# A four-layer graph network on one core: other lengths, due times and look-ahead in the plan that orders its instructions

## The chip, the cores and the metric

The kernel runs on one core of a Trainium2 chip. The metric is the device time of one execution in microseconds (us). A core has five engines that run side by side: PE multiplies matrices (and transposes by multiplying with the identity), DVE and ACT work elementwise, POOL (GpSimd) too, more slowly, and SP only issues transfers (DMAs). Each engine takes its instructions strictly in the order in which the program puts them, and waits on semaphores for the others.

## The reference, cut to what matters

x holds 32 graphs of 512 nodes with 128 features. Four layers follow one another, each of this form:

```python
h = jnp.maximum(_layernorm(x, axis=-1), 0.0)
x = x + _L0_gnn_ref(h, adj, ...)      # then L1, L2, L3 in the same way
```

Layer 0 is an attention whose scores come from pairs of nodes (node 2m and 2m+1 give the score of entry m), so small columns of h must be moved between partitions. Layers 1 and 2 are attentions with a row score plus a column score, a leaky slope, a softmax and a product with h; layer 1 adds a product with the adjacency matrix, two norms and two dense products. Layer 3 multiplies by an attention matrix that depends only on adj and on one vector of weights: it is the same for all graphs and is computed once. The graphs are independent of each other; within a graph the four layers are a chain.

## The kernel before, in words

**Tiling.** A graph is held as 128 partitions by 4 chunks by 128 features. All 32 graphs stay in `xs` on the chip. Everything that depends on adj or on weights alone is made once: the opening block (adjacency transposed and turned into masks; lines 440 to 497), `prepare()` (layers 1 and 2: folded weights, centred rows, the adjacency with its diagonal) and `prepare_last()` (layer 3's matrix, `offT` and `adiag`, lines 1072 and on: masks at L1108, counts at L1126, membership `in_row` at L1185, products at L1212, L1225 and L1259, the diagonal at L1297).

**The plan.** The order of the instructions is not that of the code. Each step is handed to `op(engine, length, emit, reads, writes, ...)` with a length in microseconds that the author measured or guessed, and `Plan.run()` plays the whole kernel through as a list schedule: it keeps a clock for each engine, takes the operation that can begin first (within `SLACK`, the one with the earliest turn), emits it, and moves on. The emitted order is then fixed by dependencies. The plan's lengths are never seen by the chip; they only decide the order on each engine. Where they are wrong, an engine is made to wait at an instruction whose input is late, and everything behind it on that engine waits too.

**What the plan reckons.** An operation ends at its length, and its reader may begin `DELAY` later. A load of data holds a modelled bus for `load` microseconds; transfers take up some of eight lanes. When the plan sees PE idle for more than `PAUSE` it puts in filler transposes (`idle_products`, L334) that keep PE busy and compute nothing.

**Turns.** Each layer of each graph is a chain with a begin time: layer 0 of graph n, layer 1 of graph n-6, layer 2 of graph n-12 and layer 3 of graph n-16 take turns, `GAPS` apart; the first `AHEAD` chains are `RAMP` times further apart. `PREPARED` and `FILLED` give the two preparation blocks their begin and the step by which each operation's turn rises. `AHEAD` is also how many graphs' x are loaded before the first is worked on.

**Layer 0** (from line 690). `preln` takes statistics on DVE (L511, L513), the inverse deviation on POOL (L523, L525) and then normalizes either on ACT (L541 on DVE and L545 on ACT) for the first `EARLY` graphs, or on POOL (L556 on ACT and L560 on POOL) for the rest. PE transposes and projects (L595), ACT copies `h` out (L412). Then comes the row of four small transfers, `emit_pair` (L699): SP moves two score columns of `h` to `u`, 0.5 KB each. DVE reads `u` first at L737. Exponentials follow on ACT (L777), two scalings on DVE (L805, L806), a split on ACT and POOL (L819, L820) and PE's products (L834 to L847); DVE and POOL add the result to `xs` (L853, L855, L857).

**Small values** (`small`, L308) come from one pool, `sm`, with eight buffers for each name. The plan doesn't know of that limit. Among them are the norms' `mv`, `shift` and `rstd`.

Of the kernel before, what the change touches and what calls it, by code (L numbers as in the profile page):

```python
# [28 lines left out]
F32 = mybir.dt.float32  # L29
# [8 lines left out]
P = 128  # L38
# [5 lines left out]

OLD, KEPT = 4, 1

AHEAD = 6


PE, DVE, ACT, POOL, SP = "PE", "DVE", "ACT", "POOL", "SP"  # L50

DELAY = {PE: 0.22, DVE: 0.15, ACT: 0.22, POOL: 0.13, SP: 2.2}

HOLD = 0.05

# [3 lines left out]

STRETCH = 3.7  # L60

PREPARED, FILLED = (35.0, 1.2), (109.0, 1.5)

RAMP = 4.1

PAUSE = 0.6

EARLY = 8

GAPS, LAGS = (5.3, 12.0, 6.7, 5.4), (0, 6, 12, 16)  # L70

# [40 lines left out]
class Plan:  # L112
# [17 lines left out]
    def op(self, engine, length, emit, reads=(), writes=(), load=0.0, transfers=0, port=0):  # L130
        slots = list(dict.fromkeys(v.slot for v in (*reads, *writes) if v.slot is not None))
        k = len(self.chains) - 1
        op = Operation(engine, length, emit, k, slots)
        op.load, op.transfers, op.port = load, transfers, port
        for s in slots:
            s.users += 1
        needs = {}
        for v in reads:
            needs.update(dict.fromkeys(v.writers))
        for v in writes:  # L140
            needs.update(dict.fromkeys(v.writers))
            needs.update(dict.fromkeys(v.readers))
        for v in reads:
            v.readers.append(op)
        for v in writes:
            v.writers.append(op)
        for n in needs:
            n.after.append(op)
            if n.chain == k:
                op.way = max(op.way, n.way + n.length + DELAY[n.engine])  # L150
        count, beside, begin, _ = self.chains[k]
        turn = begin + STRETCH * op.way if beside is None else beside[0] + beside[1] * count
        op.turn = (turn, len(self.ops))
        op.missing = len(needs)
        self.chains[-1][0] += 1
        self.ops.append(op)

    def run(self):
        tc, nc = self.tc, self.tc.nc
        idle = dict.fromkeys(DELAY, 0.0)  # L160
        bus = 0.0
        lanes = [0.0] * LANES

        held = {DVE: [], POOL: []}
        ready = {e: [] for e in DELAY}
        for op in self.ops:
# [9 lines left out]
        for _ in range(len(self.ops)):  # L176
            while oldest < len(normal) and not left[normal[oldest]]:
                oldest += 1
            best = None
            for engine, ops in ready.items():  # L180
                could = []
                for op in ops:
                    k = op.chain
                    beside = self.chains[k][1] is not None
                    if not beside and order[k] >= oldest + WINDOW:
                        continue
                    begin = max(idle[engine], op.ready)
                    if op.transfers:
                        begin = max(begin, lanes[op.transfers - 1])
                    if op.port:  # L190
                        for a, b in held[POOL if engine is DVE else DVE]:
                            if a <= begin < b:
                                begin = b
                    new = [s for s in op.slots if s.tile is None]
                    rooms = {}
                    for s in new:
                        rooms[s.room] = rooms.get(s.room, 0) + 1
                    for room, n in rooms.items():
                        if len(room.free) < n + (room.reserve if beside else KEPT if order[k] >= oldest + OLD else 0):
                            begin = None  # L200
                            break
                        begin = max(begin, sorted(room.free)[n - 1])
                    if begin is not None:
                        could.append((begin, op.turn, op))
                if could:
                    first = min(c[0] for c in could)
                    c = min((c for c in could if c[0] <= first + SLACK), key=lambda c: c[1])
                    if best is None or c[0] < best[0]:
                        best = c
            assert best is not None, "no operation can begin"  # L210
            begin, _, op = best
            if op.engine is PE and idle[PE] and begin - idle[PE] > PAUSE:
                wanted = sum(s.tile is None and s.room is self.banks for s in op.slots)
                if sum(free <= idle[PE] for free in self.banks.free) > wanted:
                    self.idle_products(begin - idle[PE])
            ready[op.engine].remove(op)
            for s in op.slots:
                if s.tile is None:
                    s.room.free.remove(min(s.room.free))
                    s.tile = s.room.make(s.name)  # L220
            end = begin + op.length
            idle[op.engine] = end
            if op.port:
                piece = op.length / op.port
                held[op.engine] = [(begin + k * piece, begin + (k + 1) * piece - HOLD) for k in range(op.port)]
            done = end + DELAY[op.engine]
            if op.load:
                bus = max(done, bus) + op.load
                done = bus
            if op.transfers:  # L230
                lanes = lanes[op.transfers :] + [done] * op.transfers
            op.emit()
            traced = nc.cur_bb.bb.instructions
            while seen < len(traced):
                ins = traced[seen]
                seen += 1
                if ins.engine in last:
                    tc.add_manual_dep(
                        ins, last[ins.engine].name,
                        mybir.DependencyInfo(mybir.DependencyClass.NoSync, mybir.DependencyReason.DATA),  # L240
                        reason="the plan's order",
                    )
                last[ins.engine] = ins
            left[op.chain] -= 1
            for s in op.slots:
                s.users -= 1
                s.until = max(s.until, done)
                if not s.users:
                    s.room.free.append(s.until)
            for n in op.after:  # L250
                n.missing -= 1
                n.ready = max(n.ready, done)
                if not n.missing:
                    ready[n.engine].append(n)
# [3 lines left out]
def kernel(  # L258
# [35 lines left out]
    KE = NE // P  # L294
    assert F == P and C == 4 and NE % P == 0 and B >= AHEAD

    cp = ctx.enter_context(tc.tile_pool(name="const", bufs=1))
    ps = ctx.enter_context(tc.tile_pool(name="ps", bufs=8, space=bass.MemoryType.PSUM))
    sm = ctx.enter_context(tc.tile_pool(name="sm", bufs=8))

    def wide(t):

        return t.rearrange("p c f -> p (c f)")

    def blk(i):
        return bass.ts(i, P)

    def small(name, shape=(P, C)):  # L308
        return sm.tile(list(shape), F32, name=name, tag=name)

    def const(name, shape, dtype=F32):
        return cp.tile(list(shape), dtype, name=name)
# [16 lines left out]
    op = plan.op  # L329
# [30 lines left out]
    xs = const("xs", (P, B, C, P))  # L360
# [12 lines left out]
    bias = const("bias", (P, C, N))  # L373
# [23 lines left out]
    v_x = [Value() for _ in range(B)]  # L397
    v_adj = [Value() for _ in range(C)]
# [5 lines left out]
    def load(dst, src, writes, size=0.0):  # L404
        op(SP, 0.5, lambda: nc.sync.dma_start(dst(), src), writes=writes, load=size, transfers=1)

    def load_x(b):
        load(lambda: xs[:, b], x[b].rearrange("(c p) f -> p c f", p=P), [v_x[b]], 1.0)

    def copy_op(engine, length, dst, src, reads, writes):  # L410
        if engine is ACT:
# [28 lines left out]
    load(lambda: wt_o.t[:, 0, :], l0_wo, [wt_o], 0.25)  # L440
    load(lambda: att, l0_att.rearrange("(t p) o -> p (t o)", p=P), [v_att])
    for ib in range(C):
        load(lambda ib=ib: bias[:, ib, :], adj[blk(ib), :], [v_adj[ib]], 1.0)
    load(lambda: wts[:, W_S, :], l0_ws, [v_wts[W_S]], 0.25)
    for b in range(1, AHEAD):
        load_x(b)
# [240 lines left out]
    def layer0(b):  # L687
        hT, _ = preln(b, ACT if b < EARLY else POOL)
        if b + AHEAD < B:
            load_x(b + AHEAD)  # L690
        h = project_scored(hT, w0_ext, [v_w0, v_w0b])
        u = Value()
# [7 lines left out]
                        u.own[up * 64 : up * 64 + 64, :, k : k + 1], h[0].t[k:P:2, up:C:2, P + k : P + k + 1]  # L700
                    )

        op(SP, 1.8, emit_pair, h, [u], transfers=4)
        sc, ls = Value(), Value()

        def emit_sc():
# [618 lines left out]
    for n, (layer, gap, b) in enumerate(order):  # L1325
        plan.chain(gap * RAMP if n < AHEAD else gap, name=layer.__name__)
        layer(b)
# [34 lines left out]
```

## Time and profile before

| what | before |
|---|---|
| median of 3 runs | 1062.99 us (1062.88 to 1063.54) |
| profiled execution: its own time | 1063.87 us |
| profiled execution: span from first to last instruction | 1062.1 us |
| mean granted clock of PE | 0.996 |
| PE busy | 1041.7 us (98%) |
| DVE busy | 868.5 us (82%) |
| ACT, POOL busy | 780.5 us, 776.2 us |
| filler transposes | 150, 19.2 us of PE |
| chain that ended last | PE 88%, DVE 4%, POOL 3% |

A busy PE is not a PE at its peak: matmuls are pipelined, and their ends are modelled. So counts of matmuls in a stretch, and the gaps between their starts, say more than busy time. A group of instructions is named by line, engine, operation and tiles (out<-in); "idle before" says how long its engine had nothing to do just ahead of it, and whose event ended that. SPq is SP's queue; a transfer's line there is its issue, and the landing is a line of its own in the chain.

### The profile page before, as it was taken

How to read it: one execution, taken by the hardware profiler on the slowest of the kernel's cores; microseconds unless marked ns; L12 is line 12 of the kernel's file. 1: busy time of each engine (PE TensorE's matmuls, PEld its weight loads, DVE VectorE, ACT ScalarE, POOL GpSimd, SP SyncE). 2: the span in 40 equal slices, each digit the busy share in tenths (PEclk: the TensorE clock that was granted, in tenths of full speed). 3: DMA queues.
4: the chain of work that ended last, by engine and by line, in shares of the span. 5: the costliest groups of instructions: out<-in, count | busy, mean ns of one | idle time of the engine just before them, and what ended most of it. 6: DMA issues, size and time to landing. Idle time of an engine off the chain costs nothing.

```text
span 1062.1 us, 25166 instructions
## 1 busy us (share of the span) xinstructions
PE 1041.7 (98%) x8475; PEld 966.0 (91%) x8475; DVE 868.5 (82%) x3694; ACT 780.5 (73%) x2024; POOL 776.2 (73%) x1140
## 2 busy tenths in 40 slices
PE   7899999999999999999999999999999999999998
PEld 7789789989999999999999999999899999999997
DVE  7799999989988878888888888888888877766752
ACT  6768897789877777777877777787777777767751
POOL 4489577778787777787778778777877666576772
PEclk9899999999999999999999999999999999999999
DMA  6400000000010000000000000000000000000001
GB/s 181 96 12 2 1 2 21 2 12 11 2 31 2 21 21 21 22 21 12 2 12 11 12 12 12 11 2 11 12 11 11 11 11 11 11 22 11 22 24 37
DMA packets 56912, 20.49 MB, mean 19 GB/s; under 512 B 21584, under 2 KB 56272, under 8 KB 56784
## 3 DMA queue, kind: packets, MB, share of 16 engines
q1 hardware_dynamic: 56784, 18.90, 7.2%
q8 instruction: 67, 1.10, 0.5%
q14 instruction: 61, 0.50, 0.2%
HBM read 10.43 MB, written 8.39 MB: 18 GB/s over the span
## 4 chain that ended last, share of the span: by engine, by line
PE 88%; DVE 4%; POOL 3%; DMA 1%; SPq 1%; issue 1%; ACT 1%; POOLq 0%; DVEq 0%; ACTq 0%
PE po L675 20%; PE pt L421 16%; PE po L984 10%; PE pg L911 10%; PE proj L595 7%; PE po L837 5%; PE prow L421 3%; PE p L581 3%; PE pz L581 3%; PE px L581 3%; PE po L980 3%; PE po L842 2%; PE po L834 1%; PE po L847 1%; POOL xn L560 1%
## 5 line engine op out<-in xcount | busy, mean ns | idle before, releaser
L675 PE MATMUL po<-h,pT 128*128 128x128 f32 x2048 | 242.8, 275 | 0.8 <-DVE pT L664 0.8
L675 PEld LDWEIGHTS po<-h,pT 128*128 128x128 f32 x2048 | 236.4, 192 | 5.8 <-issue 4.1
L560 POOL TENSOR_SCALAR xn<-xs,shift,rstd 128x128 f32<-128x128 f32 x480 | 213.1, 459 | 2.8 <-DVE top L633 0.9
L655 ACT ACTIVATE y<-y,nmax 128x512 f32<-128x512 f32 x256 | 181.7, 714 | 5.3 <-DVE nmax L637 4.6
L525 POOL TENSOR_TENSOR rstd<-ve,mhalf 128x4 f32<-128x4 f32 x160 | 170.9, 1068 | 13.3
L622 DVE CUSTOM_DVE_ANT_0 y<-prow,bias 128x512 f32<-128x512 f32 x256 | 162.8, 683 | 1.6 <-PE prow L421 1.6
L984 PE MATMUL po<-h,offT 128*128 128x128 f32 x1024 | 135.4, 275 | 0.0
L911 PE MATMUL pg<-adjTe,hg 128*128 128x512 f32 x256 | 131.0, 593 | 0.0
L421 PE MATMUL pt<-ident,y 128*128 128x128 f32 x1024 | 130.2, 274 | 0.7 <-ACT hl L819 0.7
L421 PEld LDWEIGHTS pt<-ident,y 128*128 128x128 f32 x1024 | 115.1, 141 | 13.8 <-issue 8.5
L984 PEld LDWEIGHTS po<-h,offT 128*128 128x128 f32 x1024 | 124.6, 192 | 0.0
L511 DVE BATCH_NORM_STATS2 st<-xs 128x6 f32<-128x128 f32 x512 | 109.8, 277 | 7.2 <-POOL xs L962 4.5
L595 PEld LDWEIGHTS proj<-w_ext,hT 128*128 128x128 f32 x768 | 96.8, 192 | 19.0 <-issue 9.6
L595 PE MATMUL proj<-w_ext,hT 128*128 128x130 f32 x768 | 102.9, 277 | 1.4 <-ACT hT L570 1.3
L647 ACT ACTIVATE y<-y,src 128x512 f32<-128x512 f32 x128 | 84.6, 714 | 20.8 <-DVE rmax L622 19.6
L962 POOL TENSOR_TENSOR xs<-xs,em 128x512 f32<-128x512 f32 x32 | 42.0, 1312 | 76.8 <-DVE em L961 63.8
L956 POOL TENSOR_TENSOR v<-v,rows 128x512 f32<-128x512 f32 x32 | 40.9, 1279 | 72.4 <-DVE v L955 72.4
L570 ACT ACTIVATE hT<-pt 128x512 f32<-128x512 f32 x128 | 73.5, 589 | 25.3 <-PE pt L421 14.0
L647 ACT ACTIVATE y<-y,h 128x512 f32<-128x512 f32 x128 | 84.7, 714 | 7.9 <-DVE rmax L622 7.7
L664 DVE TENSOR_TENSOR pT<-pt,adjT 128x512 f32<-128x512 f32 x128 | 82.6, 681 | 5.7 <-PE pt L421 5.6
L421 PE MATMUL pt<-ident,xn 128*128 128x128 f32 x512 | 77.8, 274 | 1.5 <-POOL xn L560 1.3
L412 ACT COPY h<-proj 128x260 f32<-128x260 f32 x192 | 66.1, 371 | 13.4 <-PE proj L595 12.4
(204 smaller groups left out, 2302.3 us busy)
## 6 DMA issues: line engine op xcount, KB each, us to landing
xs<-in_x_dram SPq DMA_DIRECT2D x32, 256.0 KB, 4.0
out_dram<-yo SPq DMA_DIRECT2D x32, 256.0 KB, 2.3
u<-h SPq DMA_DIRECT2D x128, 0.5 KB, 1.8
bias<-in_adj_dram SPq DMA_DIRECT2D x4, 256.0 KB, 4.4
wts<-in_L_gnn_W_dram SPq DMA_DIRECT2D x3, 64.0 KB, 4.2
rows<-in_L_gnn_bias_dram SPq DMA_DIRECT2D x2, 64.0 KB, 3.7
wt_o<-L_gnn_others_weight_dram SPq DMA_DIRECT2D x1, 64.0 KB, 2.5
wts<-n_L_gnn_self_weight_dram SPq DMA_DIRECT2D x1, 64.0 KB, 4.5
```

Source lines behind the costliest of these rows:

```text
L421: nc.tensor.transpose(dst(k), src(k), ident)
L511: nc.vector.bn_stats(st[:, c, :], src(c))
L525: nc.gpsimd.tensor_tensor(rstd.own, ve, mhalf, ALU.pow)
L560: nc.gpsimd.tensor_scalar(xn.t[:, c, :], src[:, c, :], shift.own[:, c : c + 1], rstd.own[:, c : c + 1], ALU.add, ALU.mult,)
L581: nc.tensor.matmul(pt.t[:, c, :], lhsT=column(hT, c), rhs=w, start=True, stop=True)
L595: nc.tensor.matmul(p[:, c, :], lhsT=column(hT, 2 * k + c), rhs=w_ext, start=True, stop=True)
L622: nc.vector.tensor_tensor_reduce(wide(y[ib].t), wide(prow.t), bias[:, ib, :], 1.0, LOWEST, ALU.add, ALU.max, rmax.own[:, ib : ib + 1],)
L647: nc.scalar.activation(yw, yw, AF.Prelu, alpha=0.2, bias=src()[:, ib : ib + 1])
L655: nc.scalar.activation(yw, yw, AF.Exp, bias=nmax.own[:, ib : ib + 1], accum_out=ssum[0].own[:, ib : ib + 1])
L675: nc.tensor.matmul(po[ib].t[:, ib, :], lhsT=pT.t[:, jb, :], rhs=h[0].t[:, jb, 0:P], start=(jb == 0), stop=(jb == C - 1),)
L911: nc.tensor.matmul(wide(pg.t), lhsT=hg.t[:, nb, :], rhs=adjTe[:, nb, :], start=(nb == 0), stop=(nb == C - 1))
L984: nc.tensor.matmul(po[ib].t[:, ib, :], lhsT=offT[:, jb, blk(ib)], rhs=h1.t[:, jb, :], start=False, stop=(jb == C - 1),)
```

## The change

Nothing is computed differently. Seven numbers of the plan change, a delay of its own is given to rows of small transfers, and the norms' small values get a pool of their own:

```diff
-AHEAD = 6
+AHEAD = 5
+PAIRED = 1.4
-PREPARED, FILLED = (35.0, 1.2), (109.0, 1.5)
-
-RAMP = 4.1
+PREPARED, FILLED = (37.0, 1.3), (160.0, 1.3)
+
+RAMP = 4.7
-EARLY = 8
+EARLY = 12
...
-            done = end + DELAY[op.engine]
+            done = end + (PAIRED if op.transfers > 1 else DELAY[op.engine])
...
+    sm_norm = ctx.enter_context(tc.tile_pool(name="sm_norm", bufs=14))
...
-        return sm.tile(list(shape), F32, name=name, tag=name)
+        pool = sm_norm if name in ("shift", "mv", "rstd") else sm
+        return pool.tile(list(shape), F32, name=name, tag=name)
...
-        load(lambda: xs[:, b], x[b].rearrange("(c p) f -> p c f", p=P), [v_x[b]], 1.0)
+        load(lambda: xs[:, b], x[b].rearrange("(c p) f -> p c f", p=P), [v_x[b]], 1.35)
...
-        load(lambda ib=ib: bias[:, ib, :], adj[blk(ib), :], [v_adj[ib]], 1.0)
+        load(lambda ib=ib: bias[:, ib, :], adj[blk(ib), :], [v_adj[ib]], 1.35)
...
-        op(SP, 1.8, emit_pair, h, [u], transfers=4)
+        op(SP, 2.6, emit_pair, h, [u], transfers=4)
```

In the plan a row of four transfers holds SP for 2.6 us instead of 1.8, and its reader may begin 1.4 us after it instead of 2.2 (`DELAY[SP]`). A load of one graph's x, or of a quarter of the adjacency matrix, holds the modelled bus for 1.35 us instead of 1.0. Five graphs are loaded ahead instead of six. `EARLY` makes ACT normalize layer 0 for the first twelve graphs instead of eight. The two preparation blocks come due later. As the list schedule depends on all of these together, the order on every engine differs from early on; PE's last 312 rows of order (equal neighbours counted as one row) are the same in both programs.

## The prediction

> **What bounds the kernel now.** I read the busy shares first, then the windows of the span, then DVE's waits in the first 60 us, then the chain of waits there.
>
> ```profile
> span 1062.1 us, 25166 instructions
> PE 1041.7 (98%) x8475; PEld 966.0 (91%) x8475; DVE 868.5 (82%) x3694; ACT 780.5 (73%) x2024; POOL 776.2 (73%) x1140
> ```
>
> PE is busy for 98% of the span. The busy time includes 150 filler transposes (row L334: 19.2 us) and matmuls that are stretched, so the stretches matter more (columns: us, busy and count of PE, PEld, DVE, ACT, POOL; clock; DMA share; GB/s):
>
> ```profile
> 0.00:20.00 20.00, 14.64 (x114) 13.63 (x115) 13.84 (x88) 10.93 (x25) 9.47 (x22) 1.00 0.71 186
> 20.00:40.00 20.00, 17.75 (x151) 16.19 (x150) 16.82 (x107) 16.28 (x55) 8.64 (x13) 1.00 0.56 133
> 40.00:60.00 20.00, 16.78 (x111) 15.77 (x112) 15.01 (x91) 14.54 (x50) 10.95 (x18) 0.83 0.22 50
> 60.00:80.00 20.00, 18.73 (x153) 17.06 (x152) 18.10 (x84) 10.98 (x38) 19.32 (x31) 1.00 0.09 15
> 80.00:100.00 20.00, 20.00 (x178) 19.77 (x177) 19.56 (x93) 19.71 (x56) 19.49 (x33) 1.00 0.02 1
> 200.00:800.00 600.00, 599.98 (x4915) 556.74 (x4915) 511.42 (x2164) 456.91 (x1193) 465.28 (x681) 1.00 0.05 13
> ```
>
> From 200 to 800 us PE never rests and runs 8.2 matmuls a microsecond: nothing is to be had there. Before 80 us it runs 529 matmuls, 6.6 a microsecond, 131 of them fillers. The start is the only place with room, apart from the drain. Who is late there?
>
> ```profile
> DVE lt L737 <- DMA u<-h: 4.7, 3, 2.5
> DVE st L511 <- DMA xs<-in_x_dram: 2.6, 1, 2.6
> DVE edge L459 <- DMA bias<-in_adj_dram: 1.3, 1, 1.3
> ```
>
> ```profile
> 27.39 3.02 SPq L699 DMA_DIRECT2D u<-h  x4
> 33.99 2.55 SPq L699 DMA_DIRECT2D u<-h  x4
> 38.85 2.74 SPq L699 DMA_DIRECT2D u<-h  x4
> ```
>
> ```profile
> 40.98 3.28 DMA u<-h
> 44.38 0.16 DVE lt L737
> ```
>
> DVE stands still three times (0.91, 1.27, 2.55 us by its timeline) because the row of four small transfers of layer 0 (L699) lands later than the plan thought. SP needs 2.6 to 3.0 us to issue a row; the plan reckons 1.8.
>
> [...] 0.6 us of SP for each L699 transfer, then a median of 1.8 us to landing. [...] behind the wait of 2.55 us at 41.8 us DVE ran nothing. [...] The trace shows clock 0.83 in 40 to 60 us, after thin PE work. [...] here the start is DVE's and the rest PE's.
>
> **The yardstick.** I add up the queues in the order in which each built program puts them, every instruction at the mean of its row in this trace (PE at its cadence in a full stretch: 0.109 us a transpose pass, 0.223 for a two-pass 128-column matmul, 0.86 for a 512-column one of L911). Where PE waits for DVE's n-th instruction, DVE's sum up to n less PE's sum so far is DVE's lead; the largest lead plus DVE's own idle time is what PE loses. Before: PE's sum 1024.3 us; largest lead 11.4 us (120 us into PE's work, at about 145 us); DVE's idle by then 14.6 us. 1024.3 + 11.4 + 14.6 = 1050.3; the other 11.8 us to the span of 1062.1 are 4.4 us after the last matmul and small stalls that I carry over unchanged. The profiled execution took 1063.87 us (1.8 more than its span); the median is 1062.99, 0.9 above the span. I convert by adding 0.9.
>
> **The change, part by part.**
>
> *PAIRED 1.4, row of four 2.6 instead of 1.8; x and adjacency loads 1.35 instead of 1.0.* No instruction is added; the order changes. The plan's old sum for a row was 1.8 + 2.2 = 4.0 us and the new one 2.6 + 1.4 = 4.0, but SP is now held for 2.6, as measured. In SP's order there stood 18, 4 and 4 loads between the first rows; now 20, 3 and 3 (layer 3's own four loads stay among the first of these, so their rows wait behind them as before). At the measured 0.59 us a load (10.6 us for 18) the second row starts about 1.1 us later, near 28, and lands near 33. DVE's first reader of rows 2 to 6 now stands behind 29.7, 34.8, 38.9, 44.5 and 48.1 us of DVE work (before 25.2, 30.6, 35.0, 44.0, 62.3). With the unavoidable 5.6 us of idle at the start DVE gets there at 35, 40, 44.5, 50 and 54 us. By the same working the rows land at 33, 37, 41.5, 46.5 and 54: of 4.7 us of waiting about 0.3 is left. Gain 4.4 us. Bounds: nothing (a row whose h is late, as then DVE waits all the same) and 4.7. What is late next is PE's or ACT's hand-over around 80 us.
>
> *Fillers.* They follow from the plan: 131 in the start become 100 (19 in the drain stay). 31 x 0.109 = 3.4 us less in PE's queue: PE's sum is 1020.9. This is a gain only if nothing real waits there instead.
>
> *PREPARED, FILLED, RAMP, AHEAD.* They move layer 3's preparation back: in DVE's order the first in_row (L1185) stands behind 83.6 us of work, before 49.3; the last diagonal (L1297) behind 154.8, before 122.5. Graph work moves ahead of it. The same DVE work is merely spread, but DVE stays ahead of PE's needs for longer: the largest lead grows from 11.4 to 13.8 us and lies at 152 us of PE work instead of 120. Cost 2.4 us; and DVE's idle, which grew by 1.4 us between 145 and 178 us, counts up to the later point: cost 1.4 us. AHEAD 5 issues each x load one graph later; layer 0's first wait for x was only the first load (2.6 us), so zero. Cover: x(1) to x(4) are issued before 8 us, long before use. Without cover a load shows 4.0 us.
>
> *EARLY 12.* Four more norms of layer 0 go from POOL to ACT: POOL loses 16 x 0.444 = 7.1 us, ACT gains 16 x 0.409 less 4 x 0.205 = 5.7 us, DVE gets four shifts at 0.08 = 0.3 us (in PE's lead above). POOL was full from 60 to 100 us, ACT only in 80 to 100. DVE idled 2.9 us between 60 and 80, when POOL led the chain. I take no gain; bounds are 2.9 us gained and the loss in the rival below.
>
> *Own room of 14.* Before, ACT's shift waited 9.6 us for POOL's xn, three times, all beyond 200 us, where ACT has slack. So zero before; it keeps norms begun earlier from waiting for eight-deep room. Cover: PE's full queue. Bounds zero to 1 us gained in the start.
>
> *Drain.* PE's last 312 rows of order, from 791.5 us on, are the same in both. Zero.
>
> **Sum.** 1020.9 + 13.8 + (14.6 - 4.4 + 1.4) + 11.8 = 1058.1 us of span, 4.0 under 1062.1. With 0.9: **1059.0 us**. Low end of this case: POOL's 2.9 us also go, 1056; high end: half of the row waits stay, 1061.
>
> **Rivals.** A, larger gain (0.14): the row waits, POOL's 2.9 us and half of the 6.8 us of half-rate clock (at most 3.4 us) go together; 1059.0 - 2.9 - 2.5 = 1053.5. For it: POOL led the chain from 57 to 74 us; against it: DVE's larger lead hides PE's clock. B, nothing moves (0.22): the rows wait for h rather than for SP, and DVE idles 14.6 + 1.4 as before: 1059.0 + 4.4 = 1063.4. For it: the fourth reader's h depends on ACT's queue of exponentials; the orders name the same handovers. C, ACT becomes the bound (0.15, slower): four more norms of 1.6 us stand in ACT's queue before the products at 60.8 us of PE work, and ACT's sum there is 1.3 us above PE's. Before, ACT had idled 28.2 us by 80 us, since it waits for others. To keep my forecast it may idle 24. Each further microsecond is one of PE; from about 30 the kernel is slower. With 33: 60.8 + 1.3 + 33 puts PE at 95 us there, 34.3 us lost, and DVE's lead grows by another 0.5: 1020.9 + 34.8 + 11.8 = 1067.5, and 1068.4 with 0.9. Against it: ACT's idle came mostly from DVE's waits, which shrink.
>
> **Numbers.** Forecast 0.49, A 0.14, B 0.22, C 0.15. About 0.2% (2.1 us) is what a measurement of this kernel can tell from no change. Faster is under 1060.9: most of the forecast (0.46) and A, with a little of B (0.02): 0.62. Within 0.2%: B 0.17, forecast 0.03, C 0.02: 0.22. Slower: C 0.13 and B's upper part 0.03: 0.16. The range leaves out one in ten at each end: half of A below, most of C above: 1053 to 1066.
>
> **What would show it.** Right: DVE's waits for u under 1 us in the first 60; fewer than 110 fillers in the start; POOL under 18 of 20 us busy in 60 to 80; from about 90 us PE full. DVE at 98% up to about 180 us. Wrong: waits for u of 4 us or more, ACT waiting long for DVE's nmax or PE's proj in 40 to 80, or PE idle after 100 us.

## The result, and the profile after

| | before | after |
|---|---|---|
| median of 20 runs each | 1063.09 us (1061.44 to 1064.45) | 1065.45 us (1064.33 to 1066.53) |
| profiled execution: own time, span | 1063.87, 1062.1 us | 1065.6, 1063.9 us |
| filler transposes | 150 | 119 |
| one round of four layers, between 375 and 750 us | 31.15 us | 31.55 us |

The changed kernel takes 1.0022 times as long (95% interval 1.0016 to 1.0029): 0.22% slower. The interval lies above 1, and the difference is about the 0.2% that the prediction took as the least that can be told from no change. The forecast was 1059.0 us, faster.

The busy shares of the changed kernel tell nothing of a loss:

```profile
span 1063.9 us, 25092 instructions
PE 1043.8 (98%) x8444; PEld 960.4 (90%) x8444; DVE 886.4 (83%) x3698; ACT 789.0 (74%) x2036; POOL 773.4 (73%) x1124
```

Its windows are the first thing that does (columns as in the prediction):

```profile
0.00:20.00 20.00, 14.79 (x119) 14.00 (x119) 12.69 (x75) 8.21 (x17) 7.29 (x20) 1.00 0.63 166
20.00:40.00 20.00, 18.32 (x147) 15.84 (x145) 19.69 (x129) 18.81 (x62) 12.88 (x20) 1.00 0.64 149
40.00:60.00 20.00, 18.46 (x152) 17.09 (x152) 18.67 (x120) 18.30 (x66) 15.36 (x26) 1.00 0.20 42
60.00:80.00 20.00, 16.48 (x127) 15.08 (x126) 18.64 (x89) 18.38 (x56) 19.18 (x31) 0.94 0.07 15
80.00:100.00 20.00, 20.00 (x164) 18.81 (x164) 16.32 (x75) 11.27 (x31) 16.52 (x26) 0.98 0.04 2
200.00:800.00 600.00, 599.63 (x4874) 551.40 (x4873) 528.17 (x2159) 457.44 (x1188) 469.31 (x681) 1.00 0.06 13
```

The first 60 us are fuller on DVE (51.1 us of 60, before 45.7) and ACT (45.3, before 41.8). But in the last line PE runs 4874 matmuls, where it ran 4915 before, in the stretch where the prediction had seen nothing to be had or lost. PE's busy time there fell by only 0.35 us. The weight loads' (PEld) fell by 5.3 us, from 556.74 to 551.40. The trace shows how a short wait hides in PE's busy time. The first of eight matmuls of `p` (L585, at 514.47 us, more of it below) starts 0.55 us after the matmul ahead of it, where 0.43 us is usual; the record of that one, 0.59 us long, covers the gap. The first matmul's own record is 0.38 us instead of 0.275; its weight load starts with it, where those of the other seven start 0.11 us ahead of theirs. So the mean of `p` between 400 and 750 us is 288 ns, where it was 275, and no idle time shows.

DVE's waits in the start went as forecast. Of those for transfers in the first 60 us, the ones for `u` (4.7 us before) are gone; only these two are left:

```profile
DVE st L515 <- DMA xs<-in_x_dram: 2.6, 1, 2.6
DVE edge L463 <- DMA bias<-in_adj_dram: 1.4, 1, 1.4
```

To see where time goes in a PE that is always busy I count its *work*: each matmul at the usual distance to the next one (the 20th percentile for its kind in that trace), fillers left out. What is left of a window is loss. (With kinds taken by line, tiles and shape, the levels move by up to 3 us; the loss between 400 and 800 us comes out the same within 0.1 us.)

| PE's work done by (us) | 100 | 200 | 300 | 400 | 500 | 600 | 700 | 800 |
|---|---|---|---|---|---|---|---|---|
| before | 62.9 | 156.7 | 254.7 | 352.9 | 451.5 | 550.0 | 648.6 | 747.3 |
| after | 65.4 | 158.9 | 257.3 | 355.6 | 453.0 | 550.5 | 647.7 | 745.1 |

The changed kernel is 2.6 us ahead at 300 us and 2.2 us behind at 800. It gives back about 4.9 us between 400 and 800, evenly, since from there on the plan's order repeats: one round of layers 0 to 3. In the timeline of PE the same product comes back after 31.55 us:

```profile
499.81 0.39 PE L838 MATMUL po<-wts,hT 128*128 128x128 f32 x2
...
531.36 0.39 PE L838 MATMUL po<-wts,hT 128*128 128x128 f32 x2
```

Before, it comes back after 31.15 us (499.59 to 530.74). The 12 rounds from 375 to 750 us are alike within 0.1 us in both traces, and 12 times 0.4 us is 4.8 us.

What is in the round? The waits between 400 and 750 us (11 rounds) of the changed kernel have these lines (total, times, longest):

```profile
PEld p L585 <- ACT hT L574: 8.7, 11, 0.8
...
PEld proj L599 <- ACT hT L574: 2.9, 11, 0.3
```

Before, there was one such wait and none for `p`:

```profile
PEld proj L595 <- ACT hT L570: 2.6, 11, 0.2
```

What such a wait cost PE is read from the starts of its matmuls, and this one cost nothing: in each of the 11 rounds `proj` starts 0.43 us after the matmul ahead of it (`pg`), the usual distance. `hT` is what ACT makes of PE's transposes of a normalized graph (`pt<-ident,xn`), and `proj` and `p` read it. PE's timeline of one round after (start, duration):

```profile
510.53 0.60 PE L425 MATMUL pt<-ident,xn 128*128 128x128 f32 x4
510.96 1.06 PE L585 MATMUL pz<-wz,ginT 128*128 128x128 f32 x8
511.86 0.60 PE L425 MATMUL pt<-ident,xn 128*128 128x128 f32 x4
512.49 1.16 PE L599 MATMUL proj<-w_ext,hT 128*128 128x130 f32 x8
513.48 1.02 PE L915 MATMUL pg<-adjTe,hg 128*128 128x512 f32 x2
514.47 1.16 PE L585 MATMUL p<-wts,hT 128*128 128x128 f32 x8
```

and ACT's in the same stretch:

```profile
511.56 0.37 ACT L856 COPY rest<-po 128x256 f32<-128x256 f32 x1 [0.27 <-DVE xs L859]
511.83 0.60 ACT L574 ACTIVATE hT<-pt 128x512 f32<-128x512 f32 x1
512.32 0.72 ACT L651 ACTIVATE y<-y,src 128x512 f32<-128x512 f32 x1
512.93 0.72 ACT L964 ACTIVATE em<-v,minus 128x512 f32<-128x512 f32 x1
513.54 0.37 ACT L416 COPY h<-proj 128x260 f32<-128x260 f32 x1
513.80 0.62 ACT L574 ACTIVATE hT<-pt 128x512 f32<-128x512 f32 x1
```

The first `hT` stands behind `rest`, which waits for DVE until 511.56; it is done at 512.43, and `proj` starts at 512.49. The second `hT` has its transposes soon after 512.3, but in ACT's order it stands behind `y`, `em` and `h`; it is done at 514.42, and `p` starts at 514.47.

ACT's queue alone does not explain it. Before, PE came to `p` later; in the built program it reads the `hT` whose transposes are the first of these lines (those at 518.30 belong to layer 0's `proj` at 524.08):

```profile
515.57 0.60 PE L421 MATMUL pt<-ident,xn 128*128 128x128 f32 x4
...
518.30 0.60 PE L421 MATMUL pt<-ident,xn 128*128 128x128 f32 x4
...
520.50 1.06 PE L581 MATMUL p<-wts,hT 128*128 128x128 f32 x8
```

```profile
519.68 1.06 ACT L570 ACTIVATE hT<-pt 128x512 f32<-128x512 f32 x2
```

The first of these two `hT` is done near 520.26, 4.7 us after its transposes began; in the changed kernel it takes 2.6 us (511.86 to 514.42). So at this place ACT was later before, and it cost nothing, because PE had 4.9 us of work from the start of the transposes to `p`. Now it has 2.2 us (transposes 0.44, `proj` 0.89, `pg` 0.86). For `proj` the same work fell from 2.2 us (512.49 to 514.68) to 1.8, while its `hT` comes 1.9 us after the transposes began instead of 1.5. The new order of PE brings the readers of `hT` closer to their transposes than ACT's order can serve them.

By the distances between matmuls, per round: transposes to `proj` +0.19 us, within `proj` +0.10, `pg` to `p` +0.13, within `p` +0.10, less 0.13 lost before between two groups of `pt<-ident,y` and no longer now: 0.39 us.

### The profile page after: what moved, and what is told of

Same layout as the page of the kernel before. It is cut to its first block, busy times and chain, and to the rows that moved or that the text cites. A ratio compares the mean times of both kernels' runs of the same rounds, so it can differ in the third digit from the quotient of the medians.

```text
span 1063.9 us, 25092 instructions
## 1 busy us (share of the span) xinstructions
PE 1043.8 (98%) x8444; PEld 960.4 (90%) x8444; DVE 886.4 (83%) x3698; ACT 789.0 (74%) x2036; POOL 773.4 (73%) x1124
## 4 chain that ended last, share of the span: by engine, by line
PE 87%; DVE 6%; POOL 3%; ACT 2%; issue 2%; DMA 0%; SPq 0%; POOLq 0%; DVEq 0%; ACTq 0%
PE po L679 20%; PE pt L425 16%; PE po L988 10%; PE pg L915 10%; PE proj L599 8%; PE po L841 4%; PE prow L425 3%; PE p L585 3%; PE po L984 3%; PE pz L585 3%; PE px L585 2%; PE po L846 2%; DVE st L515 1%; PE po L851 1%; PE po L838 1%
## 5 line engine op out<-in xcount | busy, mean ns | idle before, releaser
L564 POOL TENSOR_SCALAR xn<-xs,shift,rstd 128x128 f32<-128x128 f32 x464 | 217.3, 486 | 4.3 <-PE pt L425 3.1
L529 POOL TENSOR_TENSOR rstd<-ve,mhalf 128x4 f32<-128x4 f32 x160 | 165.2, 1033 | 13.4
L527 POOL TENSOR_SCALAR ve<-mv 128x4 f32<-128x4 f32 x160 | 41.8, 261 | 73.7 <-DVE mv L517 41.5
L574 ACT ACTIVATE hT<-pt 128x512 f32<-128x512 f32 x128 | 76.2, 595 | 24.3 <-PE pt L425 11.9
```

The costliest lines, as they stand in the source:

```text
L529: nc.gpsimd.tensor_tensor(rstd.own, ve, mhalf, ALU.pow)
L564: nc.gpsimd.tensor_scalar(xn.t[:, c, :], src[:, c, :], shift.own[:, c : c + 1], rstd.own[:, c : c + 1], ALU.add, ALU.mult,)
```

## Experiments

Each time below is the median, beside the kernel before in the same batch (1062.5 to 1062.8 us). "Before" and "after" as starts or rounds mean PE's order there.

### The start against the round

To part the two, the plan's lengths of the row of `u` switch at graph 12. In the built program PE's first 1052 instructions are then those of the changed kernel and the round is that of the kernel before; the second kernel is made the other way about.

```diff
-        op(SP, 2.6, emit_pair, h, [u], transfers=4)
+        late = b >= 12
+        op(SP, 1.8 if late else 2.6, emit_pair, h, [u], transfers=4)
+        plan.ops[-1].landing = 2.2 if late else PAIRED
...
-            done = end + (PAIRED if op.transfers > 1 else DELAY[op.engine])
+            done = end + (op.landing or DELAY[op.engine])
```

> The changed kernel, but from graph 12 on the plan reckons the row of u as before (1.8 and 2.2). PE's order is that of the changed kernel for its first 1052 instructions (about 175 us) and then repeats the round of the kernel before. Theory R (the start gained about 2.5 us, and the new repeating round gives back 0.39 us a round, about 5 us in all): 1060.5 us, period of a round 31.15 us, PE 2 to 3 us of work ahead of the kernel before at 200 us and still at 700. Rival S (the start itself, with four more norms on ACT, costs what is lost, and the round is as good as the old): 1065 us or more.

> The kernel before with its own start, and the new lengths of the row of u (2.6 and 1.4) only from graph 12 on; own room for the norms' small values. PE's order is that of the kernel before for 1078 instructions and then repeats the changed kernel's round. Theory R: 1063.1 + 4.8 = 1068 us, period 31.5 us. Rival S: 1063 us, period 31.15.

| start | round before | round after |
|---|---|---|
| before | 1062.8 | 1069.8 (ratio 1.0062, 1.0049 to 1.0074) |
| after | 1060.2 (ratio 0.9976, 0.9967 to 0.9985) | 1065.45 (beside 1063.1) |

Taken against the kernel before in its own batch, the four stand at 0, +7.0, -2.6 and +2.4 us. So the round costs 5.0 us with the new start and 7.0 with the old one; the start gains 2.6 us with the old round and 4.7 with the new one. The rival that put the loss into the start is out. The periods are 31.15 and 31.55 us as expected. The kernel of new start and old round has PE's work back in its windows:

```profile
200.00:800.00 600.00, 599.95 (x4911) 556.56 (x4911) 513.30 (x2169) 457.25 (x1194) 465.51 (x680) 1.00 0.06 13
```

and the other one, with the old start, has the changed kernel's waits:

```profile
PEld p L586 <- ACT hT L575: 8.7, 11, 0.8
...
PEld proj L600 <- ACT hT L575: 2.8, 11, 0.3
```

It is 1.8 us slower than I expected. The profiled executions of it and of the kernel before took 1069.0 and 1063.9 us, 5.2 apart, so these traces hold little more than the round's loss, and the remainder stays open.

### Why the round changed

The new lengths, 2.6 + 1.4, are the old sum, 1.8 + 2.2. But the plan uses a length twice. Its clock adds `PAIRED` (L228); the due time ("turn") of all that comes behind the row in its layer still adds `DELAY[SP]` (L152): 2.6 + 2.2 = 4.8 us instead of 4.0, times `STRETCH` 3.7, so 3.0 us later for the rest of layer 0. The test mends only this:

```diff
-                op.way = max(op.way, n.way + n.length + DELAY[n.engine])
+                op.way = max(op.way, n.way + n.length + (PAIRED if n.transfers > 1 else DELAY[n.engine]))
```

> The changed kernel, but the due times of what follows a row of u count its landing as 1.4 too, as the plan's clock does (2.6 + 1.4 = 4.0 as before, instead of 2.6 + 2.2 = 4.8 times the stretch of 3.7). PE's order repeats the round of the kernel before; the start is another (124 start fillers). Theory R: a period of 31.15 us and, if that start is worth half of the changed one, 1062 us (1060.5 to 1063.5). Rival S (it is ACT's load in the start): 1065, since EARLY stays at 12.

1060.3 us (ratio 0.9977, 0.9969 to 0.9984), period 31.15. So this one line, which the change did not touch, decides the round; the time came out at the first experiment's 1060.2, with another start (work by 300 us 257.5). A dip of PE's granted clock does not show in this comparison: the first experiment's kernel has 0.93 between 60 and 80 us, the means over the profiled executions are 0.998 there and 0.999 here, and the medians are 1060.2 and 1060.3 us.

The other test leaves the due times and gives the plan ACT's `hT` at the length of its record:

```diff
-        op(ACT, 0.49, lambda: nc.scalar.activation(wide(hT.t), wide(pt.t), AF.Relu), [pt], [hT])
+        op(ACT, 0.6, lambda: nc.scalar.activation(wide(hT.t), wide(pt.t), AF.Relu), [pt], [hT])
```

> The changed kernel, but the plan reckons ACT's hT at 0.60 us, as the trace shows it (0.58 to 0.61), instead of 0.49. The due times stay as in the changed kernel. Theory R, in its sharper form (PE loses where it stands behind hT because the plan thinks hT 0.1 us too short): PE's waits for hT in 400 to 750 fall from 1.1 us and the period falls from 31.5 to about 31.15: 1060 to 1062 us. If the loss of the round has another cause (DVE's longer instructions): period stays at 31.5, 1065 us.

The kernel took 1068.1 us (ratio 1.0052, 1.0038 to 1.0065), so the sum was missed, but its round agrees with the cause. `p` now comes behind `prow` and another group of transposes, 3.35 us after its own (515.82 to 519.17), its `hT` is done at 517.48, and its wait is gone. `proj` stands where it stood, and its wait has stayed:

```profile
PEld proj L599 <- ACT hT L574: 2.7, 11, 0.3
```

The period is 31.33 us: the 0.23 us that I had put down to `p` are back within 0.01, the rest is not. The time is lost elsewhere, before 300 us (work done 253.9, changed kernel 257.3).

### The parts of the start

Now each on the round of before, so that only the start differs. "Row" stands for the row's lengths up to graph 12, as in the first experiment; own room is in all.

```diff
 row alone                    before, with row
 all but row                  after, with:  op(SP, 1.8, ...) and DELAY[SP]
 all but EARLY                -EARLY = 12
                              +EARLY = 8
 all but PREPARED and so on   -PREPARED, FILLED = (37.0, 1.3), (160.0, 1.3)
                              +PREPARED, FILLED = (35.0, 1.2), (109.0, 1.5)
                              -RAMP = 4.7
                              +RAMP = 4.1
 row and EARLY                before, with row and EARLY = 12
 all but loads and AHEAD      -AHEAD = 5
                              +AHEAD = 6    (loads 1.0)
```

> The kernel before with only the row of u at 2.6 and 1.4 for graphs 0 to 11 (own room for the norms' small values too); all else, and the later rounds, as before (period 31.15). Theory L (the start's gain is the row's, as the prediction's 4.4 us had it): DVE's waits for u under 1 us, 1060.5 us or less. Rival M (the gain comes of the other constants, or of all together): waits for u gone, and yet 1062 to 1064 us, because another hand-over ends last instead.

> The changed kernel with the row of u at 1.8 and 2.2 throughout: loads of 1.35, AHEAD 5, EARLY 12, PREPARED, FILLED, RAMP and own room stay; the repeating round is that of the kernel before. Theory L: DVE waits 4 us or more for u and it takes 1063 us or more. Rival M: 1060 to 1062 us.

> The kernel of new start and old round, with EARLY back at 8: four norms of layer 0 go back from ACT to POOL. The prediction took no gain for them: 1060.2 us. If ACT's load in the start costs (the prediction's rival C): 1058 or less. If POOL's relief was worth its 2.9 us: 1063.

> The kernel of new start and old round, with PREPARED, FILLED and RAMP as before. By the prediction's sum (2.4 us for a larger lead of DVE and 1.4 us for a later decisive point) this is 3.8 us faster: 1056.4 us. If the moved preparation costs nothing: 1060.2. If it gains by leaving PE's fillers less room: 1062 or more.

> The kernel before with the row of u at 2.6 and 1.4 for graphs 0 to 11 and EARLY 12 (own room too); PREPARED, FILLED, RAMP, AHEAD and the loads as before. Beside the run with the row alone (1070.0 us) it tells what POOL's relief is worth there. Theory Q (with the row's wait gone, POOL's norms are the next that come late in 60 to 100 us): PE's wait for POOL's hl in 60 to 110 us falls from 4.9 to under 1 us and PE's work done by 100 us rises from 56 to 63 us or more; the time is then set by the unmoved preparation, 1066 to 1070. If POOL was not what was late: work by 100 us stays under 58 us.

> The kernel of new start and old round, with loads at 1.0 and AHEAD at 6 as before: row, EARLY, PREPARED, FILLED and RAMP are the new ones. The prediction took the loads and AHEAD at zero: 1060.2 us. If all constants fit only together, as the runs with one part undone suggest: 1063 to 1070.

| start | median | ratio, 95% interval | own time profiled | work by 300 us | sum of the two |
|---|---|---|---|---|---|
| before | 1063.1 | | 1063.9 | 254.7 | 1318.6 |
| all parts (1st experiment) | 1060.2 | 0.9976, 0.9967 to 0.9985 | 1061.7 | 256.7 | 1318.4 |
| row alone | 1070.0 | 1.0065, 1.0053 to 1.0077 | 1070.3 | 247.9 | 1318.2 |
| all but row | 1064.2 | 1.0018, 1.0012 to 1.0025 | 1067.0 | 250.9 | 1317.9 |
| all but EARLY | 1069.6 | 1.0069, 1.0057 to 1.0081 | 1069.6 | 248.3 | 1317.9 |
| all but PREPARED, FILLED, RAMP | 1070.3 | 1.0070, 1.0057 to 1.0083 | 1072.7 | 244.6 | 1317.3 |
| row and EARLY | 1075.7 | 1.0118, 1.0105 to 1.0131 | 1075.4 | 243.2 | 1318.6 |
| all but loads and AHEAD | 1069.8 | 1.0072, 1.0060 to 1.0085 | 1068.8 | 249.2 | 1318.1 |

The last column is the same within 1.3 us, so with this round the work done by 300 us tells the time. Neither theory for the row fits: with it alone the kernel is 7 us slower, without it (waits for `u` of 2.0 us) 4 us slower than with all. With the row alone one wait for `u` of 2.6 us was left, and another wait came up between 60 and 110 us, for POOL's `hl`:

```profile
PEld po L849 <- POOL hl L827: 4.9, 4, 2.7
```

With EARLY 12 beside it, this wait is

```profile
PEld po L849 <- POOL hl L827: 0.3, 1, 0.3
```

and PE's work by 100 us rises from 56.1 to 59.9 us, less than the 63 that I expected; the time, 1075.7 us, lies above the 1066 to 1070. In its place PE waits for ACT:

```profile
PE proj L600 <- ACT hT L575: 3.0, 1, 3.0
```

That `hT` (ACT at 81.83 us) stands behind two `e_at` of layer 3's preparation (from 78.16 us) and four `y`. With all parts but EARLY the wait for `hl` is 3.4 us. So POOL is what is late next, and with POOL relieved and the preparation not moved, ACT, as far as these orders go. With the old preparation PE is level with the full set at 100 us (65.1 and 65.8) and loses its time in 120 to 200 us. The longest wait of PE's weight loads there, which accounts for only a part of the loss, is for DVE's work for the graphs:

```profile
PEld px L586 <- DVE zn L929: 3.2, 1, 3.2
```

### Is a part's effect its own?

Each part undone costs 4 to 10 us, and all together gain only 2.6. That looks like a start in which any other order loses, so I nudged one constant at a time: three in the kernel of the first experiment, one in the kernel before.

```diff
-EARLY = 12
+EARLY = 11
...
-RAMP = 4.7
+RAMP = 4.8
...
-[v_x[b]], 1.35)
+[v_x[b]], 1.40)
-[v_adj[ib]], 1.35)
+[v_adj[ib]], 1.40)
...
-RAMP = 4.1
+RAMP = 4.0
```

> The kernel of new start and old round with EARLY 11 instead of 12: one norm of layer 0 goes back to POOL. If EARLY acts by POOL's relief (9.4 us for four norms): up to 2.4 us slower, 1060 to 1062.6. If any other order of the start costs: 1063 to 1070.

> The kernel of new start and old round with RAMP 4.8 instead of 4.7, 2% more distance between the first chains. If constants act by what they mean: 1060.2 within 1 us. If any other order of the start costs: 1063 to 1070.

> The kernel of new start and old round with the loads of x and of the adjacency reckoned at 1.40 us instead of 1.35. If constants act by what they mean: 1060.2 within 1 us. If any other order of the start costs: 1063 to 1070.

> The kernel before with RAMP 4.0 instead of 4.1; it plans 84 start fillers instead of 131. By the prediction's term for fillers (0.109 us each) 5.1 us faster: 1058. If the number of fillers says nothing of the time: 1062 or more. If any other order of the start costs: 1065 to 1072.

They took 1066.5 (ratio 1.0039, 1.0025 to 1.0053), 1060.0 (0.9976, 0.9967 to 0.9984), 1065.5 (1.0027, 1.0016 to 1.0038) and 1065.7 us (1.0030, 1.0021 to 1.0039). Their sums of time and work by 300 us are 1317.6, 1317.4, 1318.0 and 1319.1. One norm, or 0.05 us in the length of a load, costs over 5 us; 2% of RAMP cost nothing in the new start and 3 us in the old one. So a step that means next to nothing can cost 5 us by the order it makes, and the 4 to 10 us above can't be read as the worth of a part. The last one plans 84 fillers in the start instead of 131 and is 3 us slower, where my filler term wanted 5.1 us faster: the number of fillers says nothing of the time.

### A faster kernel

From graph 12 on, with the new start and the old due times, only `hT` is reckoned longer in the plan (0.6, then 0.7):

```diff
-        op(ACT, 0.49, lambda: nc.scalar.activation(wide(hT.t), wide(pt.t), AF.Relu), [pt], [hT])
+        op(ACT, 0.6 if b >= 12 else 0.49, lambda: nc.scalar.activation(wide(hT.t), wide(pt.t), AF.Relu), [pt], [hT])
```

> The kernel of new start and old round, with hT reckoned at 0.60 us for graphs 12 on: each proj of layer 2 comes behind the next graph's transposes instead of ahead of them. Theory W (PE's order in the round costs by its distance to ACT's hT): the round's waits for hT (2.6 us in 400 to 750) shrink and the period falls by 0 to 0.2 us: 1058 to 1060.5. If the round's order is worth nothing more: 1060.2.

> As the run before it, with hT at 0.70 us for graphs 12 on: the row of h and p move a further step back from their transposes. Theory W: period 31.0 to 31.15, 1058 to 1060.5 us. If another hand-over comes late in its place (pT or y): period above 31.2 and 1061 or more.

1059.95 us (ratio 0.9973, 0.9964 to 0.9982) and 1059.0 us (0.9964, 0.9953 to 0.9976), with a period falling from 31.16 to about 31.10 us from 530 us on. The second beats both kernels; against the first experiment's 1060.2 the gain is 1.2 us, of the size of the spread, so I don't claim the round's part in it. It excludes another suspicion: its DVE is busy for 528.4 us between 200 and 800 us, as in the changed kernel (528.2; before 511.4), so the mere length of DVE's work there is not what slowed that one.

## Why the prediction was wrong, point by point

- **The step that failed** is the carried-over term, the 11.8 us of "4.4 us after the last matmul and small stalls that I carry over unchanged", with its reading "From 200 to 800 us PE never rests and runs 8.2 matmuls a microsecond: nothing is to be had there". There was something to be lost. The order of the repeating round changed, and PE's stalls grew by 0.39 us a round, as PE reaches the readers of `hT` sooner after their transposes: 4.8 us by the traces, 5.0 us by the runs with the new start. With this added, 1059.0 becomes 1064.0, and 1065.45 was measured.
- **Why I missed it:** I costed PAIRED by the plan's clock (4.0 = 4.0) and not by the due times, which the same lengths feed through another line. That the diff edits one of two uses of a delay could be read from the code. And I added up queues with a mean for each row: such a sum has no place for a reader that PE reaches before ACT has come to its input. Where the order in the middle differs between two programs, the round should have been compared place by place, as the drain was.
- **The start's total** came out near: -4.0 us forecast, -2.6 and -4.7 measured with the two rounds. That is luck, as its terms did not hold, and steps that mean nothing move the start by as much.
- **Its terms** were not right. The row's 4.4 us: DVE's waits did go, but the row alone made the kernel slower by 7. (The landing of 1.8 us is the median of all rows; between 20 and 45 us, beside the loads, it was 3.1 us before and 2.6 after.) EARLY and the loads, taken at zero, and the moved preparation, taken at 3.8 us of cost, each cost 9 to 10 us when undone. The nudges show that such numbers can't be split or added. The filler term (3.4 us) found no support: with 47 fillers fewer the kernel before took 3 us longer.
- **The rivals:** the time lies between B's 1063.4 and C's 1068.4, and neither mechanism is its own. PE did come to wait for ACT, as in C, but in the repeating round; in the first 110 us its waits for `hT` stayed as they were (1.4 us, before 1.3). And things moved, against B, twice and with opposite signs. (A's terms add up to 1053.6, not 1053.5.)
- **What would show it:** waits for `u` under 1 us (none) and fewer than 110 fillers in the start (100) came true; POOL under 18 us in 60 to 80 did not (19.18), nor did DVE at 98% up to about 180 us (16.32 of 20 us in 80 to 100). The list of what would make the forecast wrong named waits in 40 to 80 us and PE idle after 100 us. ACT's longest wait for those in 40 to 80 us was 0.7 us. PE was idle for 1.5 us between 100 and 180 us, less than the 2.0 before, and for 0.4 us between 200 and 800, where it lost about 5: the sign should have been the count of matmuls, or the weight loads' busy time.

Left open: what in the order makes one start 5 us better than another a step away, beyond the waits shown; and the 1.8 us of the second experiment.

## What to carry to other kernels

Where an order repeats, compare one round before and after it place by place: 0.4 us in 31 outweighed everything that the start had won. For each reader take the work that its engine has between producing the input and reading the result: that distance, not the other engine's queue alone, says whether a wait shows (for `p` here 4.9 us before, without a wait, and 2.2 after, with 0.8 a round). A full engine can hide short waits in longer records (here 0.38 us for the first of eight matmuls, 0.275 for the others), so count instructions, or take the time between two returns of the same one. When a planning constant is changed, look for every place that uses it, and before giving a part of a start its worth, nudge a constant that shouldn't matter: what that moves is the resolution of such a reading.

## What was not expected of the hardware

A wait of PE for ACT appeared in the records as longer matmuls: eight matmuls of `p` took 1.16 us instead of 1.06, all of it in the first, while PE's busy time over 600 us stayed at 599.6. Beyond that nothing in the hardware was surprising; the stretch of the start in which PE's granted clock was 0.50 came down from 6.8 us before (47 to 54 us) to 3.4 us after (77 to 81 us).
